# A transformer block on one core: every product moved to 64 by 64 tiles of TensorE, in pairs with a row swap, and scores in two double PSUM banks

## The chip, the core and the metric

The kernel runs on one core of a Trainium2 chip. The metric is the device time of one execution in microseconds (us). TensorE (PE in the profile) multiplies matrices into PSUM, VectorE (DVE) does sums, maxima and 32 by 32 transposes, ScalarE (ACT) does exponentials and copies out of PSUM, GpSimd (POOL) scales rows in SBUF, and SyncE (SP) issues transfers.

## The reference

The input x has 8 batches of 1024 rows and 256 channels, all in float32. One block of attention and one feed-forward block follow each other:

```python
xn = layernorm(x)
q, k, v = xn @ Wq, xn @ Wk, xn @ Wv               # 16 heads of 64
s = (q @ k.T) / 8 + rel_table[clip(j - i + 16, 0, 32)]   # causal: j <= i
a = softmax(s) @ v                                 # heads joined: 1024 wide
x = x + layernorm(a @ Wp + bp)
y = layernorm(x); yp = y moved down by one row
xr = mu_r * y + (1 - mu_r) * yp;  xk = mu_k * y + (1 - mu_k) * yp
x = x + layernorm(sigmoid(xr @ W_r.T) * (relu(xk @ W_k.T)**2 @ W_v.T))
```

## The kernel before

**Work units.** A unit is one batch and one pair of heads: 64 units, `u`. For each unit the kernel makes q and k (`do_qk`, four products of 512 columns), v (`do_v`, two products), the scores of eight row tiles `tb` of 128 rows (`do_scores`), the transposed softmax (`turn` and `shuffle`, on DVE and by transfers) and the product with v (`do_av`, two groups of two row blocks each). Per batch come the projection (`project_out`) and the feed-forward part (`stages_ffn`, whose steps `s5`, `s6` and `s7` are its three products).

**How TensorE is tiled.** All products except the scores use the whole height of the array and half its width: `matmul` (line 433) and the loop of `do_av` (line 1293) issue two matmuls of 128 rows by 64 columns, one for each half of the output's partitions. Two such matmuls run side by side. The scores contract over only 64 channels, so line 1041 issues four matmuls of 64 rows by 64 columns: two heads (two row halves) by two halves of the output's partitions. Each float32 matmul of the program is two weight loads and two matmuls in the trace. In this text a *wave* is the set of matmul records that start within some 30 ns of each other: two records for the products, four for the scores.

**Scores.** A row tile with over 512 keys ("long", `tb` 4 to 7) is cut into two parts; a part's two heads lie in one two-bank PSUM tile `s` (ring `sl`, two buffers). A "short" row tile (`tb` 0 to 3) takes two single banks from the pool that the products use. A long part has one bias addition (line 1070, second part only), one maximum over both heads (line 1078) and one exponential for each head (line 1098, followed by a read of its sum). A short row tile has a bias addition, a maximum and an exponential for each head. When the exponentials are done, the PSUM space is free for another part.

**PSUM.** Eight banks: two double banks for the long scores (`s`), and four single ones, `pm`, shared by the products and the short scores. ACT or DVE empties a bank, then the next product may take it.

**Order.** Nothing is ordered by hand. Each step is a task with an engine, a cost in us, and its dependences. `Planner.simulate` lists the tasks in time, engine by engine, by priorities: late times, `RANK` (a bias for each kind of task), `SEEDS` (small random biases, one for each stretch of 34 us of planned time) and `URGENT` (what a change of TensorE's tiling is weighed at). `SWITCH = 0.09` is the time that the planner gives such a change. The program then holds a fixed order for every engine; at run time engines wait for each other by semaphores.

Of the kernel before, what the change touches and what calls it, by code (L numbers as in the profile page):

```python
# [43 lines left out]
URGENT = 1.05  # L44
# [3 lines left out]
    "pe:part.go": -0.82,  # L48
    "dve:top.go": 1.9,
    "act:exp.go": -3.14,  # L50
    "dve:bias.go": 1.02,
    "pool:do_scores.behind": 6.53,
    "act:do_scores.<lambda>": -2.87,
    "pool:do_scores.both": 6.86,
    "dve:do_scores.<lambda>": -0.11,
    "pool:do_scores.<lambda>": -4.38,
    "pool:scale.go": 6.48,
    "dve:one.go": 1.8,
    "pe:do_qk.go": -0.33,
    "act:do_qk.<lambda>": -20.88,  # L60
    "sp:shuffle.move": 21.5,
    "pe:do_v.go": 0.57,
    "act:do_v.<lambda>": 11.6,
    "sp:load_wqk.go": -9.79,
    "sp:load_wv.go": 1.65,
    "pe:do_av.go": 0.22,
    "act:save.<lambda>": -6.41,
    "sp:load_rows.<lambda>": -6.4,
    "dve:norm_stats.go": 2.38,
    "pe:one.go": -0.19,  # L70
    "dve:one.plus_old": -14.51,
    "pool:normed.power": -0.11,
    "pool:normed.go": 6.49,
    "dve:by_dma.<lambda>": -1.51,
    "sp:by_dma.leave": -24.02,
    "sp:by_dma.<lambda>": -17.77,
    "act:by_dma.place": 4.69,
    "pool:plus.go": -26.3,
    "pool:s2.<lambda>": -47.14,
    "act:s3.go": 2.12,  # L80
    "dve:s4.go": 3.56,
    "pe:s5.go": 0.53,
    "act:s5.<lambda>": 17.56,
    "pool:s5.<lambda>": -0.97,
    "pe:second.go": -2.43,
    "act:s6.<lambda>": 22.56,
    "dve:s7.<lambda>": -5.69,
    "sp:s9.<lambda>": -14.9,
    "pe:some.go": 1.42,
    "act:normed.go_edge": -15,  # L90
# [5 lines left out]
    392905, 816692, 244547, 283470, 560662, 39100, 216772, 294259, 588279, 412218,  # L96
    371534, 0, 431774, 883409, 180062, 984965, 373709, 0, 0, 0,
    763639, 658110, 822178, 930278, 665013, 718545, 0, 952361, 100832, 846644,
    0, 137572, 647438, 377597, 0, 469262, 83528, 641677, 323164, 611824,
    444950, 813510, 452093, 622742, 919130, 335621, 0, 751616, 573689, 0,  # L100
    0, 99909, 466380, 402426, 0, 986219, 146830, 82811, 0, 0,
    151578, 369797, 955240, 0, 0,
# [40 lines left out]
class Task:  # L143


    def __init__(self, eng, cost, fn, prio, mode, banks, mb):
        self.eng, self.cost, self.fn, self.prio, self.mode = eng, cost, fn, prio, mode
        self.banks, self.held, self.readers, self.mb = banks, (), [0] * banks, mb
        self.deps, self.after, self.makes, self.frees = [], [], [], []
        self.users, self.behind, self.left, self.first, self.seen = [], [], 0, 0.0, None  # L150


class Planner:
# [13 lines left out]
    def add(  # L167
# [8 lines left out]
        mode="cols",  # L176
        banks=0,
        frees=None,
        mb=0.13,
    ):  # L180
# [3 lines left out]
        t.deps = list(deps)  # L184
        if self.gate is not None:
            t.deps.append(self.gate)
# [22 lines left out]
        if frees is not None:  # L209
            t.deps.append(frees[0])  # L210
            t.frees.append(frees)
            frees[0].readers[frees[1]] += 1
# [3 lines left out]
    def simulate(self, tasks, prio, urgent=1.0, stretches=()):  # L216
# [30 lines left out]
        while len(order) < len(tasks):  # L247
# [30 lines left out]
            for u in t.users + t.behind:  # L278
                if u in t.behind:
                    at = start  # L280
                else:
                    at = end if u.eng == e and e != "sp" else seen
# [8 lines left out]
    def late(self, order, held):  # L291
# [3 lines left out]
        for t, start, stop, seen in reversed(order):  # L295
# [3 lines left out]
            for u in t.users:  # L299
                by = min(by, res[u] - (0.0 if u.eng == t.eng != "sp" else seen - stop))  # L300
# [9 lines left out]
    def run(self, rounds, urgent=1.0, rank={}, seeds=(0,)):  # L310

        new, self.tasks = self.tasks, []
        for t in new:
# [3 lines left out]
            deps.pop(t, None)  # L317
            for d in deps:
# [39 lines left out]
def tile_attn_ffn_block(  # L358
# [59 lines left out]
    bank = [ps_m.tile([P, HB], F32, name=f"pm{i}") for i in range(4)]  # L418
# [3 lines left out]
    def pm(t, i=0):  # L422

        return bank[t.held[i]]
# [4 lines left out]
    def matmul(dst, lhs, rhs, first, last):  # L429
# [4 lines left out]

    rows2 = [P, 2, C]
    R = {
        "xin": Ring(ins, rows2, "xin", 1),
# [14 lines left out]
        "sl": Ring(ps_l, [P, 2, HB], "sl", 2),  # L452
# [12 lines left out]
    for c in range(NCP):  # L465
        R["oT", c] = Ring(acts, [P, CT], f"oT{c}", HP + 1)
        R["y", c] = Ring(acts, rows2, f"y{c}", 1)
    for g in range(2):
        R["xnT", g] = Ring(acts, [P, NC, HB], f"xnT{g}", 2)

# [111 lines left out]
    def turned(dst, view, src, prio, part=None):  # L582
# [13 lines left out]
        t = add("pe", 0.88, go, r=[src], prio=prio + 0.5, banks=1)  # L596
# [95 lines left out]
    def project_out(b, c, prs, prio):  # L692
# [5 lines left out]

        def one(k):
            def go():  # L700
                for pr in prs:
                    matmul(
                        pm(t)[:, :C],
                        oT[b, pr, c].tile[:, (1 - k) * P : (2 - k) * P],
                        wp_sb[:, pr, :],
                        (pr == prs[0]),
                        (pr == prs[-1]),
                    )

            t = add(  # L710
                "pe",
                0.433 * len(prs),
                go,
                wp_done,
                r=[oT[b, pr, c] for pr in prs],
                prio=prio + 0.5,
                banks=1,
            )

            def plus_old():  # L720
                dst = y.tile[:, k, :]
                nc.vector.tensor_tensor(dst, pm(t)[:, :C], bp_bc if new else dst, ALU.add)  # L722
# [29 lines left out]
    def stages_ffn(b, c):  # L752
# [100 lines left out]
        def s5(prio):  # L853
            def go():
                for kk in range(NC):
                    for cc in range(NC):
                        matmul(
                            halves(t)[:, kk, :],
                            wkT[:, cc, kk * P : (kk + 1) * P],
                            box["xk"].tile[:, cc, :],  # L860
                            (cc == 0),
                            (cc == NC - 1),
                        )

            t = add("pe", 1.73, go, r=[box["xk"]], prio=prio + 0.5, banks=1)
# [20 lines left out]

        def second(lhs, w, prio):
            def go():
                for kk in range(2):
                    for cc in range(NC):  # L890
                        matmul(
                            halves(t)[:, kk, :],
                            lhs.tile[:, cc, kk * P : (kk + 1) * P],
                            w[:, cc, :],
                            (cc == 0),
                            (cc == NC - 1),
                        )

            t = add("pe", 1.73, go, r=[lhs], prio=prio + 0.5, banks=1)
            return t  # L900

        def s6(prio):
            t = second(box["xr"], wrT, prio)
# [4 lines left out]
                lambda: nc.scalar.activation(r.tile, halves(t), AF.Tanh, scale=0.5),  # L908
# [5 lines left out]
        def s7(prio):  # L914
            t = second(box["ka"], wvT, prio)
            f = box["f"] = box["r"]
            add(
                "dve",
                0.65,
                lambda: nc.vector.scalar_tensor_tensor(  # L920
                    f.tile, f.tile, 1.0, halves(t), ALU.add, ALU.mult
                ),
                r=[f],
                w=[f],
                frees=(t, 0),
                prio=prio - 0.3,
            )
# [15 lines left out]
        return [s0, s1, s2, s3, s4, s5, s6, s7, s8, s9]  # L943
# [7 lines left out]
    def do_qk(u, name, g, prio):  # L951
# [3 lines left out]
        if (u, name) not in qkv:  # L955
# [599 lines left out]
```

## Time and profile before

| what | value |
|---|---|
| median of 3 runs | 2192.43 us (2190.52 to 2192.93) |
| span of the profiled execution, first to last instruction | 2191.9 us |
| PE busy | 2161.1 us (99%), 21312 matmuls and as many weight loads |
| DVE busy | 1970.5 us (90%), 4460 instructions |
| ACT busy | 1377.4 us (63%) |
| POOL busy | 1526.8 us (70%) |
| mean granted TensorE clock | 0.998 |
| transfers | 388.92 MB, 73.3% of the 16 DMA engines' span |

The profile is one execution. Its span lies 0.5 us under the median of the runs, so a sum made against the span is moved by +0.5 us to stand against the median. In the profile's rows "128*64" or "64*64" is the tile of TensorE, "128x256" or "64x256" the output's shape; a matmul's duration includes its way through the array, so its start to the next wave's start is what it costs in a stream. "PEld" is the weight load, which overlaps matmuls.

### The profile page before, as it was taken

The numbers are of one execution on the slowest core, as the hardware profiler recorded it, in microseconds if no ns is written. First come the engines' busy times: TensorE is split into PE (matmuls) and PEld (weight loads), VectorE is DVE, ScalarE is ACT, GpSimd is POOL, SyncE is SP. The second block draws the span as 40 slices with busy tenths as digits, with TensorE's granted clock in tenths as the row PEclk, the third lists the DMA queues.
The fourth block names the chain that finished last, engine by engine and source line by source line (L and its number), as shares of the span: only waits on it lengthen the run. The fifth ranks groups of instructions, "written<-read, shape, count | busy, mean of one in ns | idle before, by whom it ended". The sixth has DMA issues, their size and how long they took to land.

```text
span 2191.9 us, 61295 instructions
## 1 busy us (share of the span) xinstructions
PE 2161.1 (99%) x21312; PEld 1182.6 (54%) x21312; DVE 1970.5 (90%) x4460; ACT 1377.4 (63%) x4314; POOL 1526.8 (70%) x3709
## 2 busy tenths in 40 slices
PE   7999999999999999999999999999999999999997
PEld 3455555555555555555555555555555555555565
DVE  5998999999998999998999989899889998999776
ACT  5665756666566565665656666565666756667454
POOL 4666677766786768775687766777667775687553
PEclk9999999999999999999999999999999999999999
DMA  5887877867778687776877777777787868877560
GB/s 166 193 199 184 194 175 179 202 167 181 178 179 200 166 193 177 183 189 169 196 180 188 181 189 181 170 175 192 170 190 178 198 167 198 193 177 189 131 152 25
DMA packets 272596, 388.92 MB, mean 177 GB/s; under 512 B 142624, under 2 KB 199968, under 8 KB 272160
## 3 DMA queue, kind: packets, MB, share of 16 engines
q1 hardware_dynamic: 272144, 384.87, 73.3%
q8 instruction: 170, 2.79, 0.6%
q14 instruction: 138, 1.13, 0.2%
q10 hardware_dynamic: 144, 0.14, 0.0%
HBM read 59.91 MB, written 25.29 MB: 39 GB/s over the span
## 4 chain that ended last, share of the span: by engine, by line
PE 89%; DVE 5%; DMA 1%; POOL 1%; issue 1%; ACT 1%; SPq 1%; ACTq 0%; DVEq 0%; POOLq 0%
PE pm L433 46%; PE pm L1293 21%; PE s L1041 16%; PE pm L1041 6%; DVE blocks L1207 2%; DVE nmax L1078 2%; POOL p L1186 1%; SPq L1267 1%; ACT p L1098 0%; DMA d<-blocks 0%; DVE pm L1070 0%; DMA out_dram<-r 0%; DVE s L1070 0%; DMA tab<-in_L_attn_rel_table_dram 0%; DVE y L722 0%
## 5 line engine op out<-in xcount | busy, mean ns | idle before, releaser
L1186 POOL TENSOR_SCALAR p<-p,rcp 128x512 f32<-128x512 f32 (+5 forms) x1536 | 883.9, 595 | 86.0 <-DVE rcp L1165 62.7
L1098 ACT ACTIVATE p<-s,nmax 128x512 f32<-128x512 f32 (+3 forms) x1024 | 616.0, 607 | 398.4 <-DVE nmax L1078 317.4
L1207 DVE STREAM_TRANSPOSE blocks<-p 128x256 f32<-128x256 f32 (+2 forms) x1016 | 724.2, 749 | 50.6 <-POOL p L1186 41.6
L1078 DVE TENSOR_REDUCE nmax<-s 128x2 f32<-128x1024 f32 (+3 forms) x512 | 516.7, 1009 | 33.3 <-PE s L1041 30.1
L1293 PE MATMUL pm<-d,v 128*64 128x256 f32 (+1 forms) x5120 | 523.5, 359 | 0.3 <-DMA d<-blocks 0.3
L1293 PEld LDWEIGHTS pm<-d,v 128*64 128x64 f32 x5120 | 351.8, 137 | 219.4 <-issue 39.6
L1041 PE MATMUL s<-k,q 64*64 64x512 f32 (+3 forms) x4096 | 444.3, 519 | 5.9 <-ACT p L1098 5.7
L1098 ACT ACTIVATE p<-pm,nmax 128x256 f32<-128x256 f32 (+3 forms) x512 | 270.9, 531 | 94.5 <-DVE nmax L1078 68.9
L433 PEld LDWEIGHTS pm<-wv,xnT 128*64 128x64 f32 x4096 | 226.5, 137 | 52.0 <-issue 26.9
L433 PE MATMUL pm<-wv,xnT 128*64 128x128 f32 x4096 | 248.1, 274 | 0.0
L433 PE MATMUL pm<-xnT,wk 128*64 128x512 f32 x1024 | 245.5, 600 | 0.1
L1078 DVE TENSOR_REDUCE nmax<-pm 128x1 f32<-128x256 f32 (+3 forms) x512 | 242.1, 478 | 3.4
L433 PE MATMUL pm<-xnT,wq 128*64 128x512 f32 x1024 | 244.7, 599 | 0.0
L433 PE MATMUL pm<-wp_sb,oT 128*64 128x256 f32 x2048 | 240.5, 381 | 0.7 <-ACT oT L1316 0.7
L1041 PEld LDWEIGHTS s<-k,q 64*64 64x64 f32 x4096 | 133.6, 132 | 180.2 <-issue 95.2
L1098 ACT ACTIVATION_READ_ACCUMULATOR p<-s,nmax 128x1 f32 x1024 | 206.7, 202 | 0.0
L433 PEld LDWEIGHTS pm<-wp_sb,oT 128*64 128x64 f32 x2048 | 141.6, 137 | 101.7 <-issue 25.2
L1041 PE MATMUL pm<-k,q 64*64 64x256 f32 (+3 forms) x2048 | 188.4, 438 | 0.0
L1070 DVE TENSOR_TENSOR pm<-pm,bm 128x144 f32<-128x144 f32 (+1 forms) x512 | 135.3, 298 | 38.1 <-PE pm L1041 36.9
L1140 POOL TENSOR_TENSOR rcp<-nmax 128x2 f32<-128x2 f32 x256 | 51.0, 199 | 148.5 <-DVE nmax L1078 119.0
L1155 POOL TENSOR_TENSOR tot<-tot,rcp 128x4 f32<-128x4 f32 x256 | 52.1, 203 | 146.8 <-ACT rcp L1148 139.8
L433 PEld LDWEIGHTS pm<-xnT,wq 128*64 128x64 f32 x1024 | 68.0, 137 | 129.7 <-issue 104.4
(103 smaller groups left out, 2266.2 us busy)
## 6 DMA issues: line engine op xcount, KB each, us to landing
d<-blocks SPq DMA_DIRECT2D x2032, 144.0 KB, 2.6
xin<-in_L_attn_x_dram SPq DMA_DIRECT2D x32, 256.0 KB, 3.0
wq<-in_L_attn_Wq_dram SPq DMA_DIRECT2D x128, 64.0 KB, 2.2
wk<-in_L_attn_Wk_dram SPq DMA_DIRECT2D x128, 64.0 KB, 2.2
wv<-in_L_attn_Wv_dram SPq DMA_DIRECT2D x64, 128.0 KB, 2.9
xre<-in_L_attn_x_dram SPq DMA_DIRECT2D x32, 256.0 KB, 3.0
out_dram<-r SPq DMA_DIRECT2D x32, 256.0 KB, 2.2
via_in<-st_in SPq DMA_DIRECT2D x112, 64.0 KB, 1.9
```

Of the source, the lines that this page charges most:

```text
L433: nc.tensor.matmul(dst[rows], lhs[:, rows], rhs, start=first, stop=last)
L1041: nc.tensor.matmul(s(hh)[o : o + D], q.tile[rows, tb * P + o : tb * P + o + D], k.tile[rows, c0:c1], start=True, stop=True,)
L1070: nc.vector.tensor_tensor(dst, dst, src, ALU.add)
L1078: nc.vector.tensor_reduce(nmax.tile[:, i, h0:h1], sl.tile[:, :, : c1 - c0] if sl else s(h0), AX.X, ALU.max, negate=True,)
L1098: nc.scalar.activation(ps[hh].tile[:, c0:c1], s(hh), AF.Exp, bias=nmax.tile[:, i, hh : hh + 1], scale=1.0, accum_out=tot.tile[:, i, hh : h ...
L1140: nc.gpsimd.tensor_tensor(rcp.tile[:, 0, :], m1, m0, ALU.subtract)
L1155: nc.gpsimd.tensor_tensor(tot.tile, tot.tile, rcp.tile, ALU.mult)
L1186: nc.gpsimd.tensor_scalar(p, p, rcp.tile[:, i, hh : hh + 1], 1.0, ALU.mult, ALU.mult)
L1207: nc.vector.transpose(blocks[g][:, :, s0 : s0 + 2 * tb + 1 : 2, hh, :].rearrange("p r a j -> p a r j"), p.tile[:, :n].rearrange("p (a r j) ...
L1267: nc.sync.dma_start(d.tile[r * QD : (r + 1) * QD, q].rearrange("p s h j -> p (s h j)"), blocks[g][q * QD : (q + 1) * QD, r].rearrange("p s ...
L1293: nc.tensor.matmul(dst, v[:, jt, rows], src, start=(jt == 0), stop=(jt == 2 * k + 1),)
```

## The change

All products now also use 64 by 64 tiles. A contraction over 128 rows is cut into two row halves. Two products that go to two different banks are computed together: in the first half of the work, rows 0 to 63 add into bank A and rows 64 to 127 into bank B; then they change places, rows 0 to 63 add into B and rows 64 to 127 into A. Between the halves stands a *relay*: an empty instruction (`nop`) on ACT that waits for the last matmul of the first half, and for which the first matmul of the second half waits. The planner sees the halves as two PE tasks with an ACT task between them, and may put other PE work there.

The pairs are: q with k of one half of the rows (`do_qk`), v of both halves (`do_v`), the two PSUM banks of an AV group, with each row tile's 128 columns by themselves (`do_av`: matmuls of 128 columns where most had 256), the two row tiles of a projection, xk·W_k with xr·W_r (`s5`; `s6` is gone), and the two row tiles of `s7`. The four single banks `pm` become two double ones (`pm0`, `pm1`), one for each pair in flight. All scores, short ones too, use the two `sl` buffers, with one bias addition and one maximum for both heads. `s7`'s gate on DVE is cut into two instructions. Transposes by PE (at the start and the end) stay at 128 by 64. `RANK`, `SEEDS` and `URGENT` have new values, so the order on every engine is another one.

```diff
-    bank = [ps_m.tile([P, HB], F32, name=f"pm{i}") for i in range(4)]
+    bank = [ps_m.tile([P, 2, HB], F32, name=f"pm{i}") for i in range(2)]
...
+    def pair(cost, jobs, *deps, r=(), prio=0.0):
...
+        def go(turn):
+            def run():
+                lists = jobs(lambda i: pm(first, i))
+                n = len(lists[0])
...
+                for i in range(n):
+                    for half in range(2):
+                        for r in range(2):
+                            part, dst, lhs, rhs = lists[r ^ turn][i]
+                            rows = slice(r * D, (r + 1) * D)
+                            cols = slice(half * D, (half + 1) * D)
+                            rhs = rhs[half] if isinstance(rhs, tuple) else rhs
+                            ins = nc.tensor.matmul(
+                                dst[cols],
+                                lhs[rows, cols],
+                                rhs[rows],
+                                start=(turn == 0 and i == 0),
+                                stop=(turn == 1 and i == n - 1),
+                            )
+                            if turn and "relay" in seen:
+                                order(ins, seen.pop("relay"), "the rows change places")
+                if not turn:
+                    seen["end"] = ins
+            return run
+
+        def nop():
+            seen["relay"] = nc.scalar.nop()
+            order(seen["relay"], seen["end"], "the first half is through")
+
+        first = add("pe", cost / 2, go(0), *deps, r=r, prio=prio, banks=1)
+        relay = add("act", 0.06, nop, first, prio=prio - 1)
+        second = add("pe", cost / 2, go(1), relay, r=r, prio=prio, after=first)
+        return first, second
...
+        t, _ = pair(3.44, jobs, r=[weights[u, "q"], weights[u, "k"], src], prio=prio)
...
-            sl = R["sl"](f"s_{what}_{i}") if size == "long" else None
-            keep = [sl] if sl else []
+            sl = R["sl"](f"s_{what}_{i}")
...
+            def bias():
+                dst = both()[:, :, c1 - c0 - w :]
+                nc.vector.tensor_tensor(
+                    dst, dst, bm[:, 2 * pr : 2 * pr + 2, BW - w :], ALU.add
                 )
+            def top():
+                nc.vector.tensor_reduce(
+                    nmax.tile[:, i, :], both(), AX.X, ALU.max, negate=True
+                )
...
+                for odd in range(2):
+                    w = odd ^ i
+                    dst = bank(w)[:, i * P : (i + 1) * P].rearrange("p (q j) -> p q j", j=QD)
+                    for jt in range(2 * k + 1 + odd):
+                        at = s0 + 2 * jt + 1 - odd
+                        lists[w].append(
+                            (i, dst, v[:, jt, :], tuple(d[:, :, at, hh, :] for hh in range(2)))
                         )
...
-URGENT = 1.05
+URGENT = 106.74
```

## The prediction

> **What bounds the kernel now.** I read the page's busy line first, then who PE waited for, then PE's timeline.
>
> ```profile
> PE 2161.1 (99%) x21312; PEld 1182.6 (54%) x21312; DVE 1970.5 (90%) x4460; ACT 1377.4 (63%) x4314; POOL 1526.8 (70%) x3709
> ```
> ```profile
> PE pm L433 <- ACT xin L556: 9.6, 2, 8.4
> PE s L1041 <- ACT p L1098: 5.7, 7, 2.1
> PE pm L433 <- ACT q L973: 2.4, 3, 1.6
> ```
>
> PE is busy all the time and hardly waits: its longest waits are for the first tile of x and 5.7 us for score buffers. DVE, at 90%, is the next limit. So PE's stream is the time, and the question is what it holds besides streaming. The timeline shows it; the columns are start, length, then the group and its number of records:
>
> ```profile
> 1000.44 1.92 PE L433 MATMUL pm<-wv,xnT 128*64 128x128 f32 x32
> 1002.19 5.35 PE L433 MATMUL pm<-wp_sb,oT 128*64 128x256 f32 x48
> 1007.47 0.45 PE L1041 MATMUL pm<-k,q 64*64 64x128 f32 x8
> 1007.74 1.68 PE L1041 MATMUL s<-k,q 64*64 64x448 f32 x16
> 1009.35 1.97 PE L433 MATMUL pm<-wv,xnT 128*64 128x128 f32 x32
> 1011.15 1.89 PE L433 MATMUL pm<-xnT,wk 128*64 128x512 f32 x8
> 1012.97 0.88 PE L1041 MATMUL s<-k,q 64*64 64x384 f32 x8
> 1013.77 1.94 PE L433 MATMUL pm<-xnT,wk 128*64 128x512 f32 x8
> ```
>
> The v product at 1000.44 stands between two groups of its own tiling: from start to start it takes 1.75 us. At 1009.35 it follows scores and takes 1.80. The 512-column group at 1011.15 precedes scores and takes 1.82 where four waves of 427 ns need 1.71. Wave by wave in the trace: a wave of c columns takes c/1.2 ns and 2.3 to 2.7 ns more, in both tilings. After a change of tiling the first wave takes 53 ns more, and the wave before it 102 ns (to 64*64) or 112 ns (from it). So a change costs 156 or 166 ns, mean 161.
>
> The span as a sum, from the matmul records: 8.4 us ahead of the first wave; pure streaming of all columns 2038; 9120 waves at 2.5 ns, 22.8; 570 changes (285 each way) at 161 ns, 91.7; 9.7 after the last wave; left over 21: two waits at the start, the slow clock of the first and last microseconds, 7 us of waits for score buffers.
>
> **The change, part by part.** The program of the changed kernel fixes each engine's order, so I counted in it.
>
> *Changes of tiling.* Only the PE transposes keep the old one: 23 changes are left of 570. 547 x 161 ns = **-88.0 us**, all on PE, with nothing beside it.
>
> *Streaming.* The same columns: 128 rows by 64 columns, two at a time, or 64 by 64, four at a time, fill the same array. Only the AV waves grow in number, from 2560 (256 and 128 columns) to 4608 (128 columns): 2048 x 2.5 ns = **+5.1**. That a 64*64 wave of 128 columns runs at 109 ns with four weight loads under it is shown by the 128-column scores; that it does so for long is not (rival B).
>
> *Relays.* 451. PE's stream to an ACT instruction that waited for it takes 212 ns (v, q and k copies), ACT's end to PE 53 ns (score buffers), and the first wave after a pause 53 more: 0.32 us with nothing between. In the order 6 have nothing between the halves and 8 more under 0.45 us; the median cover is 2.5 us of other PE work. 6 x 0.32 + 8 x 0.1 = 2.7. The `nop` queues on ACT behind what it holds (mean 0.32 us), which matters for the 66 relays with under 1 us: between 0 and 66 x 0.32 = 21, and I take little of it, since ACT idles 37% of the time. Queued behind the `nop` are exponentials, and PE waits for those through the `sl` buffers. Together **+4** (0 to 24).
>
> *PSUM buffers.* Now 768 score parts share two slots. A slot is held for 214 ns (to DVE), the bias (452 ns), the maximum (1210 ns at two times 512, 412 at two times 128), 94 ns (DVE to ACT), two exponentials with their sums (each 687+202 at 512 columns) and 53 ns. I compared each such sum with the PE work that the order puts between a part and the next but one. Slack under zero: 62 of 766, after earlier stalls are counted **+31** (16 in the first five units, 15 in all the rest); the median slack is 1.27 us. The same arithmetic on the kernel before gives 4.1 us, and its trace shows 7.3, which go: **-7**. The two double banks (copies of 2 x 0.6, against the PE work before the next pair) come short 13 times: **+5**.
>
> *Contention.* 202 parts have between 0 and 0.5 us of slack, where before it was 4. A busy DVE or ACT makes such a part late. From below: nothing. From above: a whole mean DVE instruction (1970/4460 = 0.44 us) each, 89 us. The nearest row is the kernel before: 7.3-4.1 = 3.2 us over the 24 parts with under 1 us of slack, 0.13 each; for 276 such parts 36. I take half of that, **+18**, since later parts gain what earlier ones lost.
>
> *DVE and ACT.* One bias and one maximum for two heads: biases 135.2 us to 192 x 452 + 64 x 419 ns = 113.6; maxima 242.1 to 64 x (1210+942+677+412) ns = 207.4; the cut gate +4. DVE loses 52 of 1970 us. It hides under PE, so nothing is booked; without it the contention above would be worse. ACT's 451 empty instructions are short. POOL and the transfers keep their work.
>
> *The ends.* At the end a pair must have xk and xr, and its relay has no cover, while PE idles anyway; the first and last 50 us are taken as they are: 0 (-3 to +6).
>
> Sum: 2191.9 - 88.0 + 5.1 + 4 + 31 - 7 + 5 + 18 = **2160.0**, and 0.5 to stand against the median: **2160.5 us**.
>
> **A rule of the skill that speaks against it.** In the trace the densest half microsecond of PE's queue (at 1270.1 us) holds 30 instructions, 16.7 ns each, and the densest whole one 46, 21.7 ns each. The Trainium skill, "Runtime: NRT & Kernel Launch", section on instruction fetch mechanics, says that the sequencer needs some 20 cycles for each instruction; at the 1.2 GHz that its page "TensorE: Matmul & The Clock Gate" (Part 1) gives for that sequencer, this is an estimated 16.7 ns too. By that rule alone the 128-column products would cost 160 us more and the sum would be 2320. I do not take it, since 12 instructions in 100 ns also stand in the trace, though those may have been queued.
>
> **The rivals.**
>
> *A, score buffers starve PE: slower.* The place is PE's wait before a score part, for ACT's exponential two parts back. Before, short scores had four other banks. If each of the 202 tight parts is late by a DVE instruction, contention is 89 instead of 18: 2231. It decides at 32 us more than I booked, 50/202 = 0.25 us for each tight part. For it: DVE stays over 88% busy, and fixed orders drift. Against it: the median slack of 1.27 us, and that waits were 7 us before.
>
> *B, PE's instructions come too slowly: slower.* AV (36 groups of two waves for each unit) and v (16) need 16 instructions in 219 ns, 13.7 ns each, 3328 times. At 16.7 ns a group is 267 ns: +160, 2320. It decides at +9.6 ns for each group, 14.3 ns for an instruction. Against it: a half of such a product is only 2 us long, and before it stand 512-column waves with 16 instructions in 858 ns, in which a queue fills.
>
> *C, no change.* The buffers eat the 88 us just so: 2188 to 2197, +30 on A's path.
>
> *D, better.* Plan and chip agree, no contention, half of the 36 us of buffer stalls: 2160 - 18 - 18 - 4 = 2120.
>
> That the change does not do what it says is out: the order shows 23 changes of tiling and four-way groups throughout.
>
> **How the numbers follow.** The sum's own neighbourhood, 2120 to 2185: 0.65. D's side, under 2120: 0.08. A: 0.12. B: 0.07. C: 0.06, and 0.02 lies between 2185 and 2188. A measurement of this kernel tells some 0.2% (4.4 us) from no change. Faster: 0.65 + 0.08 + 0.02 = 0.75; same 0.06; slower 0.19. The range takes D's edge and part of A: 2112 to 2212, which leaves out some 0.03 below and 0.15 above. The likeliest case's own range is 2120 to 2185.
>
> **What would show it.** PE's rows all read 64*64, except `ident`; each half of v takes 1.75 us from start to start, each half of AV 1.97. If a 128-column wave shows clearly over 109 ns, B holds. The waits of PE for `p` should come to 30 to 60 us in all, those for a relay under 10; with PE waits for `p` over 90 us, A holds. DVE busy should fall to some 1918 us. PE's summed waits of over 120 us would break the prediction; a wave cost in the products over 3 ns above c/1.2 would too.

## The result, and the profile after

The changed kernel takes **2219.92 us** (median of 4 runs, 2214.57 to 2221.1) against 2191.47 (2190.48 to 2192.93) of the kernel before on the same chip: ratio 1.0124, interval 1.0109 to 1.0138. It is slower by 28 us. The forecast was 2160.5, faster; the range reached to 2212.

The busy line of the page after:

```profile
PE 2128.7 (96%) x44352; PEld 1475.8 (67%) x44352; DVE 1967.1 (89%) x3980; ACT 1372.5 (62%) x4314; POOL 1524.1 (69%) x3709
```

PE's busy time fell by 32 us, and its share fell from 99 to 96%: PE now waits. DVE's busy time, which was to fall by 52 us, is the same. Who PE waited for, in the changed kernel (us in all, times, longest):

```profile
PE s L1121 <- ACT p L1166: 40.0, 73, 2.1
PE pm L441 <- ACT xin L616: 9.3, 2, 8.2
PE pm L473 <- DVE ka L949: 4.8, 3, 2.0
PE pm L441 <- ACT yn L616: 3.9, 1, 3.9
PE pm L473 <- ACT oT L1367: 3.1, 5, 1.0
PE pm L473 <- DVE y L787: 2.8, 6, 0.9
```

The wait for a score buffer (for the exponential that frees it) was 5.7 us and is 40.0. The wait for the first tile of x (9.3) stood there before, with 9.6. The other rows are short waits, most of them new or longer than before. None of TensorE's matmuls waits for a relay in this view; its weight loads (PEld) wait 15.9 us for relays, at 59 places, beside matmuls that may still be running. Where the idle time lies shows in the busy time by stretch; the columns are the window, its length, then the busy time of PE, PEld, DVE, ACT and POOL, the granted clock, and the share and rate of the transfers. Before:

```profile
0.00:60.00 60.00, 48.74 (x416) 22.73 (x416) 36.31 (x91) 35.96 (x96) 28.08 (x73) 1.00 0.59 169
60.00:300.00 240.00, 236.58 (x2348) 125.74 (x2344) 221.15 (x476) 154.97 (x506) 161.72 (x414) 0.99 0.81 192
300.00:2130.00 1830.00, 1826.48 (x17996) 998.11 (x17996) 1673.39 (x3773) 1156.95 (x3651) 1313.42 (x3173) 1.00 0.76 180
2130.00:2192.00 62.00, 49.25 (x560) 35.98 (x556) 39.64 (x124) 29.52 (x64) 23.55 (x50) 0.94 0.15 41
```

and after:

```profile
0.00:60.00 60.00, 41.84 (x492) 22.08 (x496) 33.48 (x73) 32.79 (x89) 26.47 (x68) 0.94 0.57 165
60.00:300.00 240.00, 229.14 (x4780) 156.78 (x4777) 210.42 (x380) 149.90 (x490) 148.70 (x390) 0.99 0.77 184
300.00:2149.00 1849.00, 1809.93 (x38257) 1264.61 (x38251) 1685.12 (x3408) 1163.92 (x3687) 1331.67 (x3214) 1.00 0.76 182
2149.00:2218.00 69.00, 47.78 (x840) 32.37 (x834) 38.04 (x122) 25.86 (x52) 17.27 (x38) 0.92 0.07 21
```

PE's idle time (length less busy) went from 11.3 + 3.4 + 3.5 + 12.8 = 31 us to 18.2 + 10.9 + 39.1 + 21.2 = 89. It grew in every stretch and most in the long middle. These rows understate it: a 512-column record lasts 0.59 us where the next wave could start after 0.43, so the first 0.16 us of each pause still count as busy.

So I did the sum of the prediction again from the matmul records. Span = streaming (columns at c/1.2 ns, 2.5 ns for each wave) + changes of tiling at 161 ns + the rest. A *pause* is time between two waves beyond that; the rows of pauses move by a few us with where a pause is taken to begin:

| us | before | after | difference |
|---|---|---|---|
| streaming | 2060.6 | 2065.7 | +5.1 |
| changes of tiling | 570: 91.8 | 23: 3.7 | -88.1 |
| pauses over 0.1 us ahead of a score wave | 7.1 | 63.3 | +56.2 |
| pauses over 0.1 us ahead of other waves | 12.4 | 32.9 | +20.5 |
| shorter pauses (12 to 100 ns) | counted in the changes | 13.3 | +13.3 |
| before the first and after the last wave | 18.1 | 16.7 | -1.4 |
| what is left over | 2.0 | 22.7 | +20.7 |
| span | 2191.9 | 2218.3 | +26.4 |

The first two rows are as forecast: -83. The rest, all that is not streaming or a change of tiling, grew from 39.6 to 148.9 us, by 109, where the forecast had booked 51. What is left over is not a view of the profile: it holds slower waves, pauses under 12 ns and the lower granted clock at both ends (0.94 and 0.92 against 1.00 and 0.94). Over the whole span the mean granted clock is 0.998 before and 0.995 after; by estimate from these two (0.2% of 2192 us against 0.5% of 2218) the clock makes at most some 7 of the 20.7 us. The shorter pauses are in part no pauses of their own: some 130 of them are the first wave after a longer pause, which takes 51 ns more.

One figure of this sum is a little high. The 161 ns of a change holds the 2.5 ns of two waves that streaming counts too. Beyond c/1.2 + 2.5 ns, a change costs 100 or 110 ns in the wave before it and 51 in the wave after, 156 at the mean. With 156 the changes are 88.9 and 3.6 us, so 85 went instead of 88, and the rest grew by some 106 us. The text below keeps the 161.

How one score pause comes about is seen in the chain that ended last, a piece of the changed kernel without its rows under 0.05 us (start us, us, what):

```profile
699.73 0.76 DVE blocks L1266
700.49 0.10 issue
700.59 0.80 DVE s L1143 x2
701.39 0.73 DVE nmax L1148
702.20 0.82 ACT p L1166 x3
703.02 0.11 issue
703.12 0.21 ACT p L1166
703.38 1.09 PE s L1121 x8
704.50 1.09 PE s L1121 x8
705.59 4.36 PE pm L473 x112
709.95 0.43 PE s L1121 x8
710.38 1.75 PE pm L473 x64
```

VectorE finishes a transpose, does two bias additions and a maximum, ScalarE an exponential and the read of its sum, and only then may PE write the next part: from 700 to 703.4 us the chain does not run over PE. PE itself streams other products meanwhile, as its timeline shows:

```profile
700.22 2.14 PE L473 MATMUL pm<-d,v 64*64 64x128 f32 x72
702.18 1.04 PE L473 MATMUL pm<-wvT,ka 64*64 64x256 f32 x16
703.38 2.21 PE L1121 MATMUL s<-k,q 64*64 64x512 f32 x15 [0.15 <-ACT p L1166]
```

The four 256-column waves at 702.18 have streamed by 703.05, so the pause is 0.33 us long, of which the view shows 0.15. Over the whole span the chain's shares are, before and after:

```profile
PE 89%; DVE 5%; DMA 1%; POOL 1%; issue 1%; ACT 1%; SPq 1%; ACTq 0%; DVEq 0%; POOLq 0%
```
```profile
PE 51%; DVE 23%; SPq 6%; DMA 6%; ACT 5%; issue 5%; POOL 4%; DVEq 0%; ACTq 0%; POOLq 0%
```

Before, PE set the pace almost alone. After, half of the chain lies on others, DVE first; that share is not idle time of PE, which works beside the chain. The last row of that piece shows also that products stream as hoped: half of v, 64 records, in 1.75 us, so a four-record wave of 128 columns costs 109 ns.

### The profile page after: what moved, and what is told of

It reads as the page before. It is cut to its first block, busy times and chain, and to the rows that moved or that the text cites. A ratio compares the mean times of both kernels' runs of the same rounds, so it can differ in the third digit from the quotient of the medians.

```text
span 2218.3 us, 107696 instructions
## 1 busy us (share of the span) xinstructions
PE 2128.7 (96%) x44352; PEld 1475.8 (67%) x44352; DVE 1967.1 (89%) x3980; ACT 1372.5 (62%) x4314; POOL 1524.1 (69%) x3709
## 4 chain that ended last, share of the span: by engine, by line
PE 51%; DVE 23%; SPq 6%; DMA 6%; ACT 5%; issue 5%; POOL 4%; DVEq 0%; ACTq 0%; POOLq 0%
PE pm L473 37%; PE s L1121 13%; DVE nmax L1148 8%; DVE blocks L1266 7%; SPq L1326 5%; ACT p L1166 4%; DVE s L1143 3%; POOL p L1245 2%; DMA xin<-in_L_attn_x_dram 1%; DMA d<-blocks 1%; PE pm L441 1%; SPq L687 1%; DVE y L787 1%; DVE xk L907 1%; DMA out_dram<-r 1%
## 5 line engine op out<-in xcount | busy, mean ns | idle before, releaser
L1166 ACT ACTIVATE p<-s,nmax 128x512 f32<-128x512 f32 (+5 forms) x1536 | 880.3, 580 | 665.3 <-DVE nmax L1148 429.6
L1148 DVE TENSOR_REDUCE nmax<-s 128x2 f32<-128x1024 f32 (+5 forms) x768 | 727.2, 950 | 76.9 <-PE s L1121 59.6
L1266 DVE STREAM_TRANSPOSE blocks<-p 128x256 f32<-128x256 f32 (+1 forms) x1016 | 738.9, 756 | 34.2 <-POOL p L1245 24.9
L1121 PE MATMUL s<-k,q 64*64 64x512 f32 (+4 forms) x6144 | 646.9, 489 | 45.9 <-ACT p L1166 40.0
L473 PEld LDWEIGHTS pm<-d,v 64*64 64x64 f32 x18432 | 543.8, 133 | 69.5 <-issue 43.8
L473 PE MATMUL pm<-d,v 64*64 64x128 f32 x18432 | 568.4, 269 | 3.0 <-DMA xin<-in_L_attn_x_dram 0.9
L473 PE MATMUL pm<-xnT,wq 64*64 64x512 f32 x2048 | 495.4, 591 | 4.3 <-DMA wq<-in_L_attn_Wq_dram 2.2
L473 PE MATMUL pm<-xnT,wk 64*64 64x512 f32 x2048 | 492.2, 591 | 0.7 <-DMA wk<-in_L_attn_Wk_dram 0.5
L1143 DVE TENSOR_TENSOR s<-s,bm 128x288 f32<-128x288 f32 (+1 forms) x512 | 227.1, 444 | 38.8 <-PE s L1121 37.2
L473 PE MATMUL pm<-wp_sb,oT 64*64 64x256 f32 x4096 | 249.4, 376 | 3.9 <-DVE r L987 1.7
L473 PE MATMUL pm<-wv,xnT 64*64 64x128 f32 x8192 | 250.7, 269 | 2.6 <-ACT oT L1367 2.2
```

Source lines behind the costliest of these rows:

```text
L473: ins = nc.tensor.matmul(dst[cols], lhs[rows, cols], rhs[rows], start=(turn == 0 and i == 0), stop=(turn == 1 and i == n - 1),)
L1121: nc.tensor.matmul(both()[o : o + D, hh, :], q.tile[rows, tb * P + o : tb * P + o + D], k.tile[rows, c0:c1], start=True, stop=True,)
L1143: nc.vector.tensor_tensor(dst, dst, bm[:, 2 * pr : 2 * pr + 2, BW - w :], ALU.add)
L1148: nc.vector.tensor_reduce(nmax.tile[:, i, :], both(), AX.X, ALU.max, negate=True)
L1166: nc.scalar.activation(ps[hh].tile[:, c0:c1], both()[:, hh, :], AF.Exp, bias=nmax.tile[:, i, hh : hh + 1], scale=1.0, accum_out=tot.tile[: ...
L1266: nc.vector.transpose(blocks[g][:, :, s0 : s0 + 2 * tb + 1 : 2, hh, :].rearrange("p r a j -> p a r j"), p.tile[:, :n].rearrange("p (a r j) ...
```

## The experiments

The theories: **slots** (the two score buffers come back late, because VectorE and ScalarE hold them), **relay** (the empty instruction and the waits at it), **order** (the planned order fits the chip badly, whichever engine is light), and later **pairs** (products in pairs wait for data and for each other). "Rest", "score pauses" and "other pauses" are the rows of the table above.

**1. Each part alone, in an order without the planner's biases.** A kernel with half of the change can't keep the order of either kernel, so four kernels were run with `RANK` empty, one seed of 0 and `URGENT = 1.0`: both kernels and each part alone.

```diff
-URGENT = 106.74
+URGENT = 1.0
-RANK = {...}
+RANK = {}
-SEEDS = (...)
+SEEDS = (0,)
```

`p_scores` is the kernel before with the new scores alone (all parts in the two `sl` buffers, one bias and one maximum for two heads):

```diff
-            sl = R["sl"](f"s_{what}_{i}") if size == "long" else None
-            keep = [sl] if sl else []
+            sl = R["sl"](f"s_{what}_{i}")
...
-                banks=0 if sl else 2,
...
-            def bias(h0, h1):
+            def bias():
+                dst = both()[:, :, c1 - c0 - w :]
```

`p_pairs` is the changed kernel with its short scores in a double bank of the products (the joined bias and maximum stay, so it is not quite the pairs alone):

```diff
-            sl = R["sl"](f"s_{what}_{i}")
+            sl = R["sl"](f"s_{what}_{i}") if size == "long" else None
...
-                return sl.tile[:, :, : c1 - c0]
+                return (sl.tile if sl else bank[t.held[0]])[:, :, : c1 - c0]
```

> The kernel before, planned without the biases by kind of task and without the random ones (all of RANK, SEEDS at nothing, URGENT 1.0): the reference point of a two by two comparison in which no order has been searched for. Slot theory (the two shared score buffers starve TensorE) and relay theory (the pairs and their relays cost) both expect some 3 to 6% over the kernel before, 2260 to 2320 us, since the order alone is worse; order theory (only the new order is at fault, not the buffers) expects this one and the changed kernel without biases to differ by the switches' gain, with the changed one some 60 us faster.

> The second part of the change alone, without biases: products stay at 128 by 64 with four single banks, but all scores use the two double buffers, with one bias addition and one maximum for both heads. No pair, no relay. Slot theory: this part carries the loss, 60 to 130 us over the unbiased kernel before. Relay theory: within 15 us of the unbiased kernel before.

> The first part of the change alone, without biases: products in 64 by 64 pairs with relays, while short scores take one of the two double banks of the products as they took single ones before (one bias addition and one maximum for both heads stay). Slot theory: 40 to 90 us faster than the unbiased changed kernel, and within 50 us of the unbiased kernel before. Relay theory: no better than the unbiased changed kernel.

> The changed kernel, planned without biases. Slot theory: slower than the unbiased kernel before by 60 to 130 us, with TensorE's waits for the score buffers over 150 us. Relay theory: slower too, but by waits ahead of the second halves of pairs. Order theory: faster than the unbiased kernel before by some 60 us.

| | us | ratio to before, interval | changes | rest | score pauses | other pauses |
|---|---|---|---|---|---|---|
| p_before | 2278.44 | 1.039, 1.0321 to 1.0458 | 740 | 102.9 | 38.8 | 25.4 |
| p_scores | 2409.02 | 1.0985, 1.0939 to 1.1031 | 946 | 197.8 | 105.6 | 30.4 |
| p_pairs | 2344.15 | 1.0689, 1.0657 to 1.0721 | few (4.0 us) | 274.4 | 79.9 | 125.7 |
| p_after | 2439.01 | 1.1122, 1.1001 to 1.1243 | few (2.7 us) | 379.6 | 183.9 | 93.2 |

The relay and the order theory fail here: `p_scores` was to lie within 15 us of `p_before` or `p_after` 60 us below it, and they lie 131 and 161 us above. The slot theory has the signs, but its bounds are passed: it allowed 130 us for `p_after`, and wanted `p_pairs` within 50 us of `p_before`, where it is 66 above. The rest is not waiting alone. The granted clock of the four profiled runs is 0.987, 0.979, 0.991 and 0.962, in the table's order, so by estimate from these and the spans a slow clock makes at most 30, 51, 21 and 93 us of the four rests.

Both parts add waits by themselves, each in its own place: the scores part makes score pauses (+67 us) and leaves the others, the pairs make the others (+100) and score pauses too (+41). The pairs also take the changes of tiling away (119 to 4 us) and lose more than they take: `p_pairs` is 66 us slower than `p_before`. And the biases are worth more than the change: 2278 to 2191 for the kernel before, 2439 to 2220 for the changed one. The size of a wait in one order says little of another.

**2. A lighter bias; a heavier relay.** From here on every kernel but `replan` and `thin_before` keeps the changed kernel's order on every engine.

```diff
-                dst = both()[:, :, c1 - c0 - w :]
+                dst = both()[:, :, c1 - c0 - 1 :]
...
-                    dst, dst, bm[:, 2 * pr : 2 * pr + 2, BW - w :], ALU.add
+                    dst, dst, bm[:, 2 * pr : 2 * pr + 2, BW - 1 :], ALU.add
```

> The changed kernel with the same order on every engine, but each bias addition covers one column of each head instead of up to 144; the rest of the bias and the mask are left out. It takes some 0.3 us out of the time that a biased part holds its score buffer and some 150 us out of VectorE's load. Slot theory: TensorE's waits ahead of score parts fall from 64 us to under 30, the whole to 2140 to 2175 us. Relay theory (waits come from the pairs' relays on ScalarE): no change, 2215 to 2222. Order theory (a fixed order that fits the chip badly): some 2200.

```diff
+    mhalf2 = const.tile([P, 2], F32, name="mhalf2")
...
             seen["relay"] = nc.scalar.nop()
             order(seen["relay"], seen["end"], "the first half is through")
+            nc.scalar.copy(mhalf2, mhalf)
```

> The changed kernel with the same order, and one small copy on ScalarE more behind every relay's nop (451 of them, some 0.1 to 0.2 us each, 45 to 90 us of ScalarE in all). Slot theory: the score buffers wait for ScalarE a little longer, 5 to 25 us more. Relay theory: at least 45 us more. Order theory: under 10.

`thin_bias`: 2216.66 us, ratio 1.0095 (1.0062 to 1.0128). VectorE is 131 us lighter (1836.3 busy), the score pauses fall from 63.3 to 51.9, and other pauses rise from 32.9 to 37.6. The slot theory had asked for far more; the time lies in the range that the relay theory gave. `relay2`: 2236.3 us, 1.0194 (1.0139 to 1.0248); 451 more small copies on ScalarE cost 16 us, 0.036 each, most of it in other pauses (42.2) and none in score pauses (62.3). The relay theory, which asked for at least 45, falls; the 16 us are inside the slot theory's 5 to 25, but they do not come by the score buffers as it argued.

**3. The relay on another engine.**

```diff
-            seen["relay"] = nc.scalar.nop()
+            seen["relay"] = nc.sync.nop()
```

> The changed kernel with its relays issued by SyncE instead of ScalarE; every engine's other instructions stay in the same order. In the changed kernel's profile ScalarE's exps wait 28.8 us for product matrices (ACT p <- PE pm), 33 times: they stand behind a relay that waits for its first half. Theory A (late exps behind relays hand the score buffers back late): those 33 waits vanish, the gaps ahead of score parts (64 us) shrink by 15 to 40 us, time 2180 to 2205. Theory B (the waits come from score parts and pairs that need each other's slots in this order, and the relay's engine is indifferent): time 2212 to 2228. Theory C (SyncE reaches its relays late because it stands behind transfers): second halves wait, time above 2235.

The same line with `nc.gpsimd.nop()`:

> The changed kernel with its relays issued by GpSimd instead of ScalarE, all else in the same order. GpSimd is busy 1524 us of 2218 with instructions of some microseconds, so a relay that comes behind one waits for its rest. Theory A (late exps behind relays): the exps come free as with SyncE, but second halves wait for GpSimd; 451 relays by some 0.2 to 0.5 us, time 2230 to 2350. Theory B (relay's engine indifferent): 2212 to 2228.

On SyncE 3201.69 us (ratio 1.4597, 1.4573 to 1.4621); on GpSimd 2225.9 us (1.0161, 1.0125 to 1.0198). PE's longest wait with the relay on SyncE:

```profile
PE pm L473 <- SPq L487: 771.8, 128, 9.9
```

PE waited up to 9.9 us for a relay on SyncE, which issues the transfers; the granted clock fell to 0.87 in that run, so the loss of 980 us is not all waiting. On GpSimd the kernel is 6 us slower than with relays on ScalarE, and the intervals overlap; it is not faster. This alone does not clear the exponentials that stand behind relays: their waits for products, which the expectation put down to relays (28.8 us, 33 times), are still 23.8 us, 26 times, so most of them were not the relays' doing. `no_swap` below, without relays, settles it.

**4. VectorE's scores work taken away; another order.**

```diff
-                    nmax.tile[:, i, :], both(), AX.X, ALU.max, negate=True
+                    nmax.tile[:, i, :], both()[:, :, c1 - c0 - 8 :], AX.X, ALU.max, negate=True
```

with the bias of `thin_bias`:

> The changed kernel with the same order on every engine; the bias works on one column per head and the maximum on the last eight columns, so most of both is left out: VectorE loses some 131 us of bias and about 600 us of maxima, and a score buffer comes back some 1 us earlier. Theory S (two score buffers held too long): the gaps ahead of score parts (64 us in the changed kernel) and what follows from them go, time 2100 to 2160. Theory O (in this order engines wait in turn, whichever is lightened): 2185 to 2216.

`replan` tells the planner a longer bias, and has new values of `RANK`, `SEEDS` and `URGENT` for it:

```diff
-                ready = add("dve", 0.07 + 2 * w / 960, bias, t, bm_done, r=[sl], prio=prio - 0.5)
+                ready = add("dve", 0.18 + 2 * w / 960, bias, t, bm_done, r=[sl], prio=prio - 0.5)
```

> The changed kernel's own tasks; only their order differs: the planner is told 0.18 instead of 0.07 us as the fixed part of a bias, since bias and the maximum behind it take 480 ns from start to start where the plan reckons 370, and its ranks and seeds are chosen anew with that. Theory M (the order that came with the change counts on a bias that is too short, and the waits come from there): time 2170 to 2200. Theory T (the waits belong to two score buffers and to pairs that hold their product buffers over two halves, whatever the order): 2205 to 2250.

`thin_scores_dve`: 2178.04 us, 0.9945 (0.9924 to 0.9967). VectorE loses 667 us. The busy line and its middle stretch:

```profile
PE 2108.9 (97%) x44352; PEld 1506.5 (69%) x44352; DVE 1299.7 (60%) x3980; ACT 1373.4 (63%) x4314; POOL 1518.4 (70%) x3709
```
```profile
300.00:2104.00 1804.00, 1786.82 (x38061) 1284.68 (x38054) 1108.49 (x3392) 1162.17 (x3676) 1320.06 (x3201) 1.00 0.77 186
```

VectorE is at 60%, and PE's idle time in the middle is 17 us where it was 39. Score pauses are 25.0 instead of 63.3, other pauses 33.1, as before. So VectorE's scores work holds up PE by some 42 us in this order; taking most of it away leaves a rest of 104. The time lies between the two theories' ranges: each has a part of it. `replan`: 2260.77 us, 1.0307 (1.0261 to 1.0353), worse than either expected; that the bias was planned too short is not shown to be the cause, and my order is no better one.

**5. Two controls.** The thin form with its relays on GpSimd, and the kernel before with the same cut of biases and maxima:

```diff
-                            dst = sl.tile[:, :, c1 - c0 - w : c1 - c0]
+                            dst = sl.tile[:, :, c1 - c0 - 1 : c1 - c0]
...
-                        sl.tile[:, :, : c1 - c0] if sl else s(h0),
+                        sl.tile[:, :, c1 - c0 - 8 : c1 - c0] if sl else s(h0)[:, c1 - c0 - 8 : c1 - c0],
```

> The run with thin biases and maxima once more (2178 us), with its relays on GpSimd; every other instruction in the same place. There ScalarE's exps waited 139.8 us for product matrices, behind relays on ScalarE. Theory E (exps held behind relays are what is left between 300 us and the tail, 38 us of TensorE waits): that stretch falls below 20, time 2150 to 2165. Theory I (the relay's engine is indifferent also when VectorE is light): 2170 to 2190.

> The kernel before with the same cut: biases on one column, maxima over the last eight columns, the rest of both left out; order unchanged. If VectorE's scores work costs TensorE time only in the changed kernel (41 us between the changed kernel and its thin form), the kernel before, whose waits other than switches are 9 us between 60 us and its tail, gives back 0 to 10 us: 2180 to 2193. If VectorE holds both kernels up alike: 2145 to 2165.

`thin_scores_pool`: 2189.82 us (0.999, 0.9971 to 1.0008): moving the relay costs 12 us and gains nothing, though the exponentials' waits for products fall from 139.8 to 16.0 us; so the exponentials behind relays are not what is left either. `thin_before`: 2184.67 us (0.9961, 0.9946 to 0.9976). The cut gives the kernel before 9 us and the changed kernel 42. VectorE was as busy before (90%) and held up little. What the rest holds in `thin_before` (29.0) and in `thin_scores_dve` (103.7) differs by 75 us with little of VectorE's scores work left, so that part does not come from this work.

**6. What the rest waits for: exps, or the swap.**

```diff
-                            part, dst, lhs, rhs = lists[r ^ turn][i]
+                            part, dst, lhs, rhs = lists[r][i]
...
-            seen["relay"] = nc.scalar.nop()
-            order(seen["relay"], seen["end"], "the first half is through")
+            seen.pop("end")
```

> The changed kernel with the row halves not swapped, so that every product adds the same half of its rows twice and no relay is needed: relays and their waits are gone, and the count and the shapes of matmuls and the order of all other work stay. Relay theory (what waits for and behind the relays is the cost): time 2160 to 2195. Buffer theory (pairs and parts hold PSUM, the relay costs a hand-over only): 2200 to 2222; doubling the relay's ScalarE part cost 16 us, so 5 to 18 us below 2220 is what I expect.

```diff
-                        ps[hh].tile[:, c0:c1],
-                        both()[:, hh, :],
+                        ps[hh].tile[:, c0 : c0 + 64],
+                        both()[:, hh, :64],
...
+                    src = ident[:, 0:1].to_broadcast([P, c1 - c0])
-                        p, p, rcp.tile[:, i, hh : hh + 1], 1.0, ALU.mult, ALU.mult
+                        p, src, rcp.tile[:, i, hh : hh + 1], 1.0, ALU.mult, ALU.mult
```

> The changed kernel with exps over 64 columns of each part (the rest of the exps left out; GpSimd's scale reads a constant of the same width instead): ScalarE loses some 400 us, a score buffer comes back 0.2 to 0.7 us sooner. If score buffers are the limit, the gaps ahead of score parts (64 us) fall below 30 and the time to 2165 to 2195; if VectorE's own queue is what makes the buffers late, exps matter little: 2200 to 2220.

`thin_both` has these exps, the one-column bias and a maximum over the first 64 columns (in `thin_scores_dve` it was the last eight).

> Thin biases, maxima and exps at once (first or last columns only; the rest left out), order as in the changed kernel. Score buffers then come back in well under half of their time. If the buffers explain what VectorE's work does not, waits outside the first 300 and the last 69 us fall from 38 us (thin biases and maxima alone) below 15 and the time to 2130 to 2160; if the rest is the pairs' own (hand-overs, ends, order of products), it stays at 2165 to 2180.

| | us | ratio to before, interval | rest | score pauses | other pauses |
|---|---|---|---|---|---|
| after | 2219.92 | 1.0124, 1.0109 to 1.0138 | 148.9 | 63.3 | 32.9 |
| no_swap | 2220.98 | 1.0125, 1.0103 to 1.0148 | 153.6 | 61.2 | 38.8 |
| thin_exp | 2209.79 | 1.0072, 1.0056 to 1.0089 | 139.0 | 39.7 | 48.0 |
| thin_scores_dve | 2178.04 | 0.9945, 0.9924 to 0.9967 | 103.7 | 25.0 | 33.1 |
| thin_both | 2171.35 | 0.9898, 0.9882 to 0.9913 | 99.4 | 16.0 | 39.1 |

`no_swap` is the clearest answer of all: without the swap, the relay and every wait at it, the time is the same to 0.1%, inside the interval; I had expected 5 to 18 us less. Its pairs still hold two banks each over both halves. The exps show how a pause moves: `thin_exp` takes 24 us from the score pauses, and 15 of it come back ahead of other products; the time stays in the range of the side that said exps matter little (2200 to 2220). With biases, maxima and exps all thin, the score pauses are nearly gone, and still 99 us of rest stand, 39 in other pauses; the time is in the range given for a rest that is the pairs' own (2165 to 2180). PE's waits in `thin_both`:

```profile
PE s L1121 <- ACT p L1166: 11.5, 15, 1.6
PE pm L441 <- ACT xin L616: 9.6, 2, 8.4
PE pm L473 <- DMA wq<-in_L_attn_Wq_dram: 6.4, 4, 3.0
PE pm L473 <- DVE ka L949: 5.4, 4, 2.0
PE pm L441 <- ACT yn L616: 3.9, 1, 3.9
PE pm L473 <- DMA d<-blocks: 3.5, 11, 0.5
```

They are for many things, weights, transposed blocks, `ka` and `yn` at the end, a few microseconds each. PE's idle time in the last 69 us is nearly the same in every thinned form (in `thin_both` 22.3 of 69, in the changed kernel 21.2): thinning the scores does not touch that part.

No form that computes the whole reference came under the kernel before.

## Why the prediction was wrong, step by step

*The removed work: right, to 3 us.* 547 changes of tiling went, and streaming rose by 5.1 us; the 83 us are in the table (80 at 156 ns a change). Rival B is dead: halves of v take 1.75 us and halves of AV 1.97 in the stream (from 700.22 to 702.18 in the rows above; at the median of 108 and 182 such halves that run unbroken). For B spoke a rule of the Trainium skill, "Runtime: NRT & Kernel Launch" (instruction fetch mechanics): the sequencer needs some 20 cycles for each instruction, from which the prediction had estimated 16.7 ns. The densest 0.5 us of PE's queue in the changed kernel holds 42 instructions, 11.9 ns each, and the densest 4 us 288, 13.9 ns each, where 16.7 ns would allow 240. Instructions that had waited in a queue could fill such a stretch too, so the trace does not settle the rule; it shows that nothing of the kind slowed these products.

*Relays, +4: right, if anything too high.* `no_swap` measures them at nothing (+1 us, inside the interval).

*PSUM buffers and contention, +31 - 7 + 18 = +42: too small, +56 measured.* This is the step that failed in kind: I took the slack of each part from the order, and let each part be late on its own. In the changed kernel's trace some 120 to 140 of 768 parts wait (by where a pause is taken to begin), 0.5 us each, not the 62 that the slack sum had; with VectorE's scores work thinned, 38 of the 63.3 us of score pauses go. My reading, which no run shows by itself, is that lateness on VectorE is not a draw for each part: a part that waits delays the matmuls behind it, these the copies, biases and maxima that VectorE meets next. I took half of the scaled price "since later parts gain what earlier ones lost"; the full one, 36, would have made 60, near the measured 56, which may be chance.

*The double banks, +5, and the ends, 0: the larger miss, and what turned the sign.* The other pauses grew by 20.5 us, shorter ones by 13.3 and what is left over by 20.7, against 5 for the double banks and the 4 of the relays. That is 45 us that stood in no term, more than the whole slots term. Of it the ends are a measured part: PE's idle time in the first 60 and the last 62 to 69 us grew from 24.0 to 39.4 us, where I had taken "0 (-3 to +6)". I priced one resource in detail, found it to be the tight one, and booked almost nothing for the rest of the order.

In sum: forecast -31.9 against the span, measured +26.4, off by 58.3. The terms: score pauses 56.2 - 42 = 14.2; other pauses 20.5 - 5 = 15.5; short pauses 13.3 - 4 = 9.3; left over 20.7; ends of the stream -1.4.

*DVE, -52: wrong, and my arithmetic was.* The rows are most of the biases of the short scores, before, and most of all biases, after:

```profile
L1070 DVE TENSOR_TENSOR pm<-pm,bm 128x144 f32<-128x144 f32 x384 | 102.9, 302 | 33.0 <-PE pm L1041 32.1 <-ACT v L1009 0.5
```
```profile
L1143 DVE TENSOR_TENSOR s<-s,bm 128x288 f32<-128x288 f32 x448 | 200.5, 448 | 36.4 <-PE s L1121 35.1 <-ACT rcp L1207 0.5
```

A row's mean is the duration of one instruction, and neighbours on VectorE overlap at their ends; sums of rows count that overlap. The timeline gives what one costs, from its start to the next start. Before:

```profile
1016.78 0.53 DVE L1070 TENSOR_TENSOR pm<-pm,bm 128x144 f32<-128x144 f32 x2 [1.02 <-PE pm L1041]
1017.22 0.70 DVE L613 STREAM_TRANSPOSE st_in<-xn 128x512 f32<-128x512 f32 x1
```

and after:

```profile
1003.05 0.43 DVE L1143 TENSOR_TENSOR s<-s,bm 128x288 f32<-128x288 f32 x1
1003.52 0.96 DVE L1148 TENSOR_REDUCE nmax<-s 128x2 f32<-128x768 f32 x1
```

Before, two biases of one head each took 0.44 us together, since VectorE went on to something else. After, one bias for both heads takes 0.47 us, because its own maximum follows at once and waits for it: 480 ns at the median in 476 of 512 cases, where a bias followed by other work takes 332 to 375 (32 cases). The kind of instruction that follows is not the reason: before, a long part's bias followed by the maximum of a short part took 364 ns at the median of 115 cases. The joined instruction saves nothing. Counted in this way, to the next start or the own end, all biases went from 216.3 to 224.0 us and all maxima from 682.2 to 672.4: +8 and -10, where the forecast had -22 and -35.

*Rival A* named the right place and the right chain. It wanted 113 us there (31 - 7 + 89, which made 2231); 56 were found, and that the time came near its 2231 is luck: it did so through the pauses that no rival had. Its sign, "PE waits for `p` over 90 us", did not show: 40.0 in the view of waits, 63.3 by the records. The forecast's own sign, 30 to 60 us of these waits, came true by the view, and the time missed all the same. *C* and *D* are out.

**What stays open.** VectorE's scores work explains some 42 us of the 109 that came back (33 more than the kernel before gives back for the same cut), the exps at most some 7 on top, the relay nothing. Of the other pauses and of the 23 us left over I can say where they lie, not what causes each. The larger part of the miss, 45 of 58 us, so has no shown cause. The pairs' hold on two banks over both halves was not thinned by itself, and it may be the cause. The experiments show only that pauses move from product to product when one cause is thinned. Whether a better order of the same tasks exists was not settled by one try.

## What to carry to other kernels

When a stream that was busy at 99% is shortened by 4%, ask first how much slack the second engine leaves: here it was at 90%, and the 83 us that were removed came back as 109 us of pauses and slower waves. Price them for all resources that the order uses, not for the tightest alone; here the full contention would have been nearer than half of it. And take an engine's saving from start to start in the timeline; sums of a row's durations count overlaps.

## What the runs showed of the hardware

- A bias addition on VectorE whose own maximum follows at once costs 480 ns from start to start; followed by other work, 332 to 375, also where that is another part's maximum (364 before). So a maximum that reads what the addition just ahead of it wrote starts some 0.12 us later.
- Four 64 by 64 tiles with 128 columns keep 109 ns for each wave over 1.75 to 1.97 us, with their weight loads hidden.
- Where the order left PE pauses, the clock fell too: in `p_after`, with 380 us of rest, the mean granted clock was 0.962, and with the relays on SyncE 0.87, against 0.998 in the kernel before.
- An empty instruction on ScalarE between two PE stages cost nothing that could be measured while PE had other work between them (+1 us when 451 of them went); on GpSimd 451 cost 12 us in the thin form, and 6, within the noise, in the full one. On SyncE, which issues the transfers (0.51 to 0.60 us for most in the changed kernel's chain at 752 to 757 us), the same one made the kernel 46% longer.
